# An edge-list kernel for four graph layers: layer 2 without its division, its norms and beta partly on GpSimd, and three tiles' gathers tied to earlier scores

## The chip, the cores and the metric

The kernel runs on one core of a Trainium2 chip. The core has a matrix engine (PE, TensorE), a vector engine (DVE, VectorE), an activation engine (ACT, ScalarE) and a general-purpose engine (POOL, GpSimd); SP (SyncE) issues most of the DMA transfers. Each engine works through its own queue in a fixed order and waits on semaphores for the others. The metric is the device time of one execution in microseconds (us), and a kernel's figure is the median of several executions.

## What is computed

Four residual graph layers on `x` of shape (8, 2048, 64) over one adjacency matrix of 2048 x 2048, which is sparse (about four neighbours for a node on average, many more for the first nodes). Each layer is `x = x + layer(max(layernorm(x), 0))`:

```python
# layer 0: dot-product attention, no weights
scores = einsum('bnd,bmd->bnm', h, h) / 8
x += softmax(where(adj > 0, scores, -1e12)) @ h
# layer 1: additive attention, elu
h1 = h @ W; e = leaky_relu(h1 @ a1 [rows] + h1 @ a2 [columns], 0.2)
x += elu(softmax(where(adj > 0, e, -9e15)) @ h1)
# layer 2: four dot-product heads with self loops, then one more such attention
def gat(h, mask, b): return softmax(where(mask, h @ h.T, -1e16)) @ h + b
z  = leaky_relu(concat_heads(gat(h @ Wh.T, adj + I, bh)), 0.2)
z2 = leaky_relu(gat(z @ Wo.T, adj + I, bo), 0.2)
x += (z2 - mean(z2)) * rsqrt(var(z2) + 1e-5) * gamma + beta
# layer 3: as layer 1, with relu in place of elu
```

A node with no neighbour at all gets the mean of all rows in layers 0, 1 and 3, since a softmax over equal masked scores is uniform.

## The kernel before

**Tiles.** The 2048 nodes are 16 tiles of 128, one node to a partition. A tile's row holds all eight batches side by side (`F` = 512 = 8 x 64). An edge list is built on the chip in layer 0 (`lists`, lines 594 to 718). After it, tile `i` has `ROWS[i]` row slots (a slot is one neighbour for each of the 128 nodes) and `PACKED[i]` packed slots, which hold the further neighbours of the nodes that have many; 0/1 matrices, `sel` and `selt`, tie a packed slot to its nodes through TensorE. `sel` lies in DRAM and is loaded again for the second attention of layer 2 (L880, one load of 2 MB).

**Tables and gathers.** Every layer writes the rows that its neighbours will need to a DRAM table (`store_rows`, L352) and then fetches a slot's 128 rows by an indirect DMA that GpSimd issues (`gather`, L244) into a ring of 26 slots. Tables 0, 1 and 4 have one more row, the mean of all rows. `store_rows` makes it: for each tile four products of 128 columns with `ones` (L357), whose sums VectorE adds to `acc` (L359, L361), and after the last tile a transpose, a copy and a DMA. A gather needs the whole table, the mean too where there is one.

**Stages and loops.** `pipeline(*stages)` calls the stages of a layer for the 16 tiles in a given `order`, a later stage one tile behind the one ahead of it. A list scheduler then fixes each engine's order from these calls and its own costs; so an edit also shifts neighbours. The stages are:
- layer 0 (0 to 365 us): lists and dot-product attention, one tile after the other, with layer 1's norm and projection behind it;
- layer 1 (365 to 595 us): additive attention, then layer 2's head projections;
- the heads of layer 2 (595 to 1152 us): `take2` gathers a tile's rows and fetches the query rows of its packed slots (`fetch`, L752, the tiles `qe`, four of them), `first2` makes scores on VectorE (L777, L781), `second2` the weighted sums (GpSimd L794 and L807, TensorE L801 and L809), `third2` and `fourth2` the output projection;
- the second attention of layer 2 (1152 to 1440 us), described next;
- layer 3 (1440 to 1595 us).

**The second attention.** For a tile, `take3` gathers its slots and loads its own rows. `first3` squares the rows on ScalarE (L889) and makes scores (L423 to L432; the tile's own score is subtracted in L894). `second3` sums the weights (S, in L902), takes their reciprocal (L903), and calls `weigh_sum`, which multiplies the gathered rows by their weights (`wg`, L381, GpSimd) and adds them up in PSUM with TensorE (`y`, L386). `third3` divides `y` by S (L472), adds the bias `bo` (L910), takes leaky relu (L445, L446) and begins the layer norm (`norm_a`: sum L261, mean L265, subtraction L268, square on ScalarE). `norm_b` (L281 to L286) ends it: a sum, then ScalarE's Ln and Exp for the reciprocal root. `fourth3` scales the tile (L292), multiplies by gamma (L918), adds beta (L919), adds to `x` (`add_store`, L486), stores `x`, and starts the layer norm for layer 3 with another `norm_a`. `pre_b`, `pre_c` (L313, four transposes L300, copy L301) and `pre_d` make layer 3's rows and store table 4.

**Small steps.** List building and the norms use many operations on 128 x 1 to 128 x 24 elements on VectorE (L645, L662, L664, L717, L718, L265, L273).

Of the kernel before, what the change touches and what calls it, by code (L numbers as in the profile page):

```python
# [65 lines left out]
def edge_stack(ctx: ExitStack, tc: tile.TileContext, x_in, adj, w1, w1t, a1, wh, wht, bh, wo, bo,  # L66
# [28 lines left out]
    nc.gpsimd.memset(eps, EPS)  # L95
    ones = const.tile([P, 1], F32, name="ones")
# [17 lines left out]
    acc = const.tile([P, F // P], F32, name="acc")  # L114

# [40 lines left out]
    bo_b, gamma_b, beta_b = (const.tile([P, D], F32, name=name) for name in ("bo_b", "gamma_b", "beta_b"))  # L156

    def weights_in(pool):
# [34 lines left out]
        for t, src in ((bo_b, bo), (gamma_b, gamma), (beta_b, beta)):  # L193
            nc.gpsimd.dma_start(out=t, in_=bass.AP(tensor=src.tensor, offset=src.offset, ap=[[0, P], [1, D]]))
# [62 lines left out]

    def norm_a(src, st, centre, eng=nc.vector):
# [4 lines left out]
        if centre:  # L263
            mean = small.tile([P, B], F32, name="ln_m")
            eng.tensor_scalar(mean, s, INV_D, None, op0=OP.mult)  # L265
            st["less"] = None
            st["src"] = rows_pool[0].tile([P, F], F32, name="ln_xc", bufs=3)
            eng.tensor_tensor(heads(st["src"]), heads(src), wide(mean), op=OP.subtract)  # L268
# [4 lines left out]
        nc.vector.tensor_scalar(st["less"], s, -INV_D, None, op0=OP.mult)  # L273
# [4 lines left out]
    def norm_b(st):  # L278
# [3 lines left out]
        nc.scalar.activation(q, q, AF.Ln, scale=INV_D, bias=eps)  # L282
# [12 lines left out]
    def transposed(src):  # L295
# [5 lines left out]
        nc.scalar.copy(t.rearrange("p k n -> p (k n)"), p)  # L301
# [5 lines left out]
    def pre_c(u, eng=None):  # L307
        def f(i, st):
# [6 lines left out]
            if u is not None:  # L315
                st["xt"] = transposed(st["xh"])
# [19 lines left out]
    def pre_d(k, u):  # L336

        def f(i, st):
# [8 lines left out]
            store_rows(k, i, xh, k != 2)  # L347
        return f

    def store_rows(k, i, xh, mean):  # L350
        cols = table[k].shape[1]
        nc.sync.dma_start(out=table[k][i * P:(i + 1) * P, :], in_=xh[:, :cols])  # L352
        if mean:
            C = F // P
            p = ps_m.tile([P, F], F32, name="m")
            for c in range(C):
                nc.tensor.matmul(p[:, c:c + 1], xh[:, c * P:(c + 1) * P], ones, start=True, stop=True)  # L357
            if i == order[0]:
                nc.vector.tensor_copy(acc, p[:, :C])  # L359
            else:  # L360
                nc.vector.tensor_tensor(acc, p[:, :C], acc, op=OP.add)  # L361
            if i == order[-1]:
                p = ps_m.tile([P, F], F32, name="m")
                nc.tensor.transpose(p[:C, :P], acc, ident)
                mr = rows_pool[0].tile([C, P], F32, name="mr", bufs=1)
                nc.vector.tensor_copy(mr, p[:C, :P])
                nc.sync.dma_start(out=table[k][N, :F].rearrange("(c p) -> c p", p=P), in_=mr)

# [4 lines left out]
    def weigh_sum(i, st, w, own=None, eng=nc.gpsimd):  # L373
# [3 lines left out]
        if own is not None:  # L377
            nc.tensor.matmul(y, ident, own, start=True, stop=False)
        for t0, m, g in rows(i, 0, n, 2):
# [133 lines left out]
    def additive(k, wd, *finish):  # L513
# [18 lines left out]
        def first(i, st):  # L532
# [6 lines left out]
            for t, m, g in rows(i, 0, K):  # L539
                nc.vector.tensor_tensor(s[:, t:t + m, :], g[:, :, F:], fs[:, None, :B].to_broadcast([P, m, B]),  # L540
                                        op=OP.add)
# [3 lines left out]
            if k == 4:  # L545
                nc.vector.tensor_tensor(s[:, :K, :], s[:, :K, :], fs[:, None, B:].to_broadcast([P, K, B]),
                                        op=OP.subtract)
# [33 lines left out]
    with tc.tile_pool(name="rows", bufs=2) as rp:  # L581
        rows_pool[0] = rp
        sel_all[0] = rp.tile([P, sum(PACKED) * P], F32, name="sel", bufs=1)
        with tc.tile_pool(name="lists", bufs=2) as pool, \
# [39 lines left out]
            def lists(i, st):  # L624
# [20 lines left out]
                nc.vector.tensor_scalar(ends, ends, LIFT, 0.0, op0=OP.subtract, op1=OP.max)  # L645
# [16 lines left out]
                nc.vector.tensor_scalar(idx[:, at:at + K], ell[:, :K], -1.0, N + 1.0, op0=OP.mult, op1=OP.add)  # L662
                if K > 1:
                    nc.vector.tensor_scalar(mba[:, at + 1:at + K], ell[:, 1:K], 0.0, NEG, op0=OP.is_equal, op1=OP.mult)  # L664
# [52 lines left out]
                nc.vector.tensor_scalar(idx[:, at + K:at + K + T], ke, -1.0, N + 1.0, op0=OP.mult, op1=OP.add)  # L717
                nc.vector.tensor_scalar(mp, mp, NEG, None, op0=OP.mult)  # L718
# [744 lines left out]
```

## Time and profile before

| what | us |
|---|---|
| median of three runs | 1600.91 (1598.85 to 1601.07) |
| the profiled execution | 1596.8 |
| its span, first to last instruction | 1595.0 |
| TensorE matmul busy in the span | 1295.0 |
| VectorE busy | 1242.0 |
| GpSimd busy | 1006.4 |
| ScalarE busy | 768.0 |
| mean granted TensorE clock (1 is full speed) | 0.899 |

The span and the profiled execution's own time differ by the 1.8 us that lie around the program. A busy time is the sum over an engine's instructions, without the issue of DMAs; where two engines are both busy, they overlap, so the column does not add up to the span. "Busy" also says nothing of what a stage waits for: that is read stage by stage, and from the chain of waits that leads to the last instruction. In lines of a group, `L472 DVE TENSOR_TENSOR y<-y,rec 128x512 ... x16 | 11.0, 690 | 2.4 <-PE y L386` means line 472 on VectorE, output and inputs, their size, sixteen instructions, 11.0 us in all, 690 ns for one, and 2.4 us of idle time of the engine ahead of them, with what ended most of it.

### The profile page before, as it was taken

What the parts mean: (1) busy time and instruction counts of PE and PEld (TensorE: products, weight loads), DVE (VectorE), ACT (ScalarE), POOL (GpSimd) and SP (SyncE); (2) the same over time, 40 slices, a digit from 0 to 9 for tenths busy, and PEclk for the clock granted to TensorE, in tenths of its full rate; (3) what the DMA queues carried; (4) which work ended last, traced back from release to release, by engine and by line L of the source; (5) the groups of instructions that cost most, each with busy time, mean ns of one, the idle gap of its engine ahead of it and who ended that gap; (6) DMA issues with size and microseconds to landing.
All of it is one profiled execution on the core that took longest, in us unless ns stands there. A gap on an engine that the chain in (4) does not pass through costs nothing.

```text
span 1595.0 us, 16633 instructions
## 1 busy us (share of the span) xinstructions
PE 1295.0 (81%) x4280; PEld 671.0 (42%) x4280; DVE 1242.0 (78%) x2489; ACT 768.0 (48%) x2475; POOL 1006.4 (63%) x844
## 2 busy tenths in 40 slices
PE   3768898995989771899987999999747788975888
PEld 1624354564544430344343444443323354563555
DVE  5998989854689776999998799871159999974666
ACT  3424555672557781465541455555424446680111
POOL 6336777766750007998789889898278486306650
PEclk9997887987999996899999999999968798957899
DMA  7775654536874449465266345400085354136761
GB/s 216 233 244 158 201 183 152 198 107 182 260 253 153 173 164 348 161 232 173 88 209 204 111 141 182 158 14 7 27 321 154 93 179 126 67 103 204 244 205 69
DMA packets 88177, 266.99 MB, mean 167 GB/s; under 512 B 14957, under 2 KB 15001, under 8 KB 79881
## 3 DMA queue, kind: packets, MB, share of 16 engines
q0 software_dynamic: 37392, 141.05, 28.3%
q1 hardware_dynamic: 50680, 124.80, 22.6%
q8 instruction: 36, 0.59, 0.2%
q14 instruction: 69, 0.56, 0.1%
HBM read 208.74 MB, written 57.05 MB: 167 GB/s over the span
## 4 chain that ended last, share of the span: by engine, by line
PE 24%; DVE 13%; POOL 8%; DMA 7%; ACT 6%; issue 5%; SPq 0%; POOLq 0%; DVEq 0%; ACTq 0%
PE y L809 10%; DMA g<-table,idx 4%; POOL wh L794 3%; POOL g L244 3%; DMA rows<-table 3%; PE y L386 3%; PE y L801 2%; PE m L846 2%; ACT yn L817 2%; PE m L858 2%; DVE s L781 2%; DVE prod L777 2%; DVE prod L423 1%; POOL wh L807 1%; PE m L842 1%
## 5 line engine op out<-in xcount | busy, mean ns | idle before, releaser
L244 POOL DMA_INDIRECT g<-table,idx x405 | 389.3, 961 | 268.3 <-issue 115.6
L794 POOL TENSOR_TENSOR wh<-g,w 128x1024 f32<-128x1024 f32 x162 | 307.2, 1918 | 35.8 <-PE y L809 33.9
L386 PE MATMUL y<-wg,ident 128*128 128x512 f32 x392 | 223.0, 696 | 22.6 <-POOL wg L381 12.7
L381 POOL TENSOR_TENSOR wg<-g,w 128x1024 f32<-128x1024 f32 (+1 forms) x91 | 156.6, 1736 | 75.2 <-ACT w L437 65.9
L781 DVE TENSOR_REDUCE s<-prod 128x32 f32<-128x2048 f32 x81 | 183.9, 2286 | 20.2 <-ACT w L783 19.8
L809 PE MATMUL y<-wh,ident 128*128 128x512 f32 x320 | 155.6, 614 | 23.7 <-POOL wh L807 21.5
L386 PE MATMUL y<-wg,selt 128*128 128x512 f32 x256 | 135.1, 634 | 4.6 <-POOL wg L381 2.9
L809 PE MATMUL y<-wh,selt 128*128 128x512 f32 x256 | 123.1, 605 | 13.2 <-POOL wh L794 13.2
L817 ACT ACTIVATE yn<-y,rec 128x64 f32<-128x64 f32 x512 | 111.3, 367 | 29.7 <-PE y L809 29.0
L386 PEld LDWEIGHTS y<-wg,ident 128*128 128x128 f32 x392 | 79.0, 219 | 106.6 <-issue 66.2
L777 DVE TENSOR_TENSOR prod<-q,g 128x2048 f32<-128x2048 f32 x49 | 111.5, 2275 | 3.7 <-ACT g L775 3.3
L381 DVE TENSOR_TENSOR wg<-g,w 128x1024 f32<-128x1024 f32 (+1 forms) x92 | 98.9, 1086 | 11.3 <-PE y L386 9.5
L443 DVE SCALAR_TENSOR_TENSOR zt<-m,bhc,att 128x512 f32<-128x512 f32 x64 | 47.1, 737 | 75.3 <-ACT att L442 75.3
L809 PEld LDWEIGHTS y<-wh,ident 128*128 128x128 f32 x320 | 59.4, 195 | 98.6 <-issue 62.4
L400 PE MATMUL m<-w,selt 128*128 128x8 f32 (+1 forms) x384 | 58.8, 255 | 50.7 <-ACT w L437 16.5
L400 PEld LDWEIGHTS m<-w,selt 128*128 128x128 f32 x384 | 60.8, 205 | 92.9 <-ACT w L437 26.8
L775 ACT COPY g<-g 128x512 f32<-128x512 f32 x81 | 50.4, 622 | 84.5 <-DVE prod L777 83.6
L429 PE MATMUL q<-rows,sel 128*128 128x512 f32 x128 | 79.8, 725 | 12.7 <-DVE prod L431 4.7
L801 PE MATMUL y<-rows,ident 128*128 128x512 f32 x128 | 70.9, 640 | 19.6 <-DMA rows<-table 14.4
L777 DVE TENSOR_TENSOR prod<-qe,g 128x2048 f32<-128x2048 f32 x32 | 73.0, 2281 | 13.9 <-DMA qe<-qtab,qidx 12.7
L357 PE MATMUL m<-ones,xh 128*128 128x1 f32 x384 | 70.6, 307 | 10.7 <-DVE idx L717 3.5
L357 PEld LDWEIGHTS m<-ones,xh 128*128 128x128 f32 x384 | 70.8, 274 | 20.0 <-issue 13.2
(221 smaller groups left out, 2673.0 us busy)
## 6 DMA issues: line engine op xcount, KB each, us to landing
qtab<-q SPq DMA_DIRECT2D x16, 1040.0 KB, 4.1
a<-in_adj_dram SPq DMA_DIRECT2D x32, 512.0 KB, 5.1
q<-qtab SPq DMA_DIRECT2D x14, 1040.0 KB, 5.3
table<-xh SPq DMA_DIRECT2D x48, 256.0 KB, 3.3
rows<-table SPq DMA_DIRECT2D x48, 256.0 KB, 4.1
xs<-x SPq DMA_DIRECT2D x48, 256.0 KB, 2.2
x<-xs SPq DMA_DIRECT2D x48, 256.0 KB, 3.3
table<-xh SPq DMA_DIRECT2D x32, 260.0 KB, 2.1
```

The source lines that it names most:

```text
L244: g = nc.gpsimd.indirect_dma_start(out=ring[:, (held[i] + t) % RING, :cols], out_offset=None, in_=table[k][:, :], in_offset=bass.IndirectO ...
L357: nc.tensor.matmul(p[:, c:c + 1], xh[:, c * P:(c + 1) * P], ones, start=True, stop=True)
L381: eng.tensor_tensor(wg[:, :m].rearrange("p t (b d) -> p t b d", b=B), g[:, :, :F].rearrange("p t (b d) -> p t b d", b=B), w[:, t0:t0 + m, ...
L386: nc.tensor.matmul(y, lhs(i, t), wg[:, t - t0, :], start=(t == 0 and own is None), stop=(t == n - 1))
L400: nc.tensor.matmul(p[:, :cols], selt(i, t), packed[:, t, :], start=(t == 0), stop=(t == T - 1))
L429: nc.tensor.matmul(qe, sel(i, t - K), q, start=True, stop=True)
L777: nc.vector.tensor_tensor(pr.rearrange("p (b h) d -> p b h d", h=H), q[:, :B * H * D].rearrange("p (b h d) -> p b h d", h=H, d=D), heads(g ...
L781: nc.vector.tensor_reduce(s[:, t - lo, :], pr, AX.X, OP.add)
L794: nc.gpsimd.tensor_tensor(wg, heads(row(i, t))[:, :, None, :].to_broadcast([P, B, 2, D]), w[:, :, 2 * k:2 * k + 2, None].to_broadcast([P, ...
L801: nc.tensor.matmul(st["ys"][j], ident, xb[:, 4 * j:4 * j + 4], start=True, stop=False)
L809: nc.tensor.matmul(st["ys"][j], lhs(i, t), wg[:, 4 * j:4 * j + 4], start=False, stop=(t == n - 1))
L817: nc.scalar.activation(yn[:, b, h, :], st["ys"][j][:, b, h, :], AF.Copy, scale=st["rec"][:, 4 * j + b, 2 * k + h:2 * k + h + 1])
```

## The change

It has five parts.

1. **Small steps.** Twelve kinds of `tensor_scalar` or `tensor_tensor` on VectorE whose operands lie in SBUF become `scalar_tensor_tensor` with the same result; the second operand is then a constant tile (`zero`, `np1`, `neg1`) read as a broadcast, or the operation itself.
2. **Means.** `store_rows` makes none. For table 0 the old way stays, called earlier. For table 1, the copy after the transposes becomes four ScalarE copies that sum as they go (`accum_out`, into `parts`), with one reduction at the end. For table 4, one product `ones` x `xh` of 1 x 512 adds up over the tiles in a PSUM bank.
3. **Second attention of layer 2.** `y` is no longer divided by S: layer norm does not depend on the scale of its input if the constant 1e-5 is scaled by S squared, and leaky relu keeps a positive factor. So `rec` is now 1e-5 x S x S, added to the variance in `norm3`, and the bias enters `y` as S x bo, by a product of the transposed S (8 x 128) with a block-diagonal `bo_d`. Beta is added to `x` by GpSimd (`beta3`) and not behind gamma, and the mean and the subtraction of the norm of `x` move to GpSimd.
4. **`sel`** is loaded in 16 pieces, each behind the load of its tile's rows.
5. **Heads.** In `take2` the first gather of the fifth, sixth and seventh tile waits for the last score of the tile four ahead.

```diff
@@ constants
+    zero, np1, neg1 = (const.tile([P, 1], F32, name=name) for name in ("zero", "np1", "neg1"))
+    for t, v in ((zero, 0.0), (np1, N + 1.0), (neg1, NEG)):
+        nc.gpsimd.memset(t, v)
+    parts = const.tile([P, NT, F // P], F32, name="parts")
@@ new helpers
+    def alike(t, like):
+        return t.to_broadcast(like.shape)
+    def times(dst, src, k):
+        nc.vector.scalar_tensor_tensor(dst, src, k, alike(zero, src), op0=OP.mult, op1=OP.add)
+    def less_from(dst, src):
+        nc.vector.scalar_tensor_tensor(dst, src, -1.0, alike(np1, src), op0=OP.mult, op1=OP.add)
@@ norm_a
-            eng.tensor_scalar(mean, s, INV_D, None, op0=OP.mult)
+            if eng is nc.vector:
+                times(mean, s, INV_D)
+            else:
+                eng.tensor_scalar(mean, s, INV_D, None, op0=OP.mult)
...
-            eng.tensor_tensor(heads(st["src"]), heads(src), wide(mean), op=OP.subtract)
+            if eng is nc.vector:
+                nc.vector.scalar_tensor_tensor(heads(st["src"]), heads(src), 1.0, wide(mean), op0=OP.mult,
+                                               op1=OP.subtract)
+            else:
+                eng.tensor_tensor(heads(st["src"]), heads(src), wide(mean), op=OP.subtract)
...
-        nc.vector.tensor_scalar(st["less"], s, -INV_D, None, op0=OP.mult)
+        times(st["less"], s, -INV_D)
@@ norm_b
-    def norm_b(st):
+    def norm_b(st, more=None):
...
-        nc.scalar.activation(q, q, AF.Ln, scale=INV_D, bias=eps)
+        if more is None:
+            nc.scalar.activation(q, q, AF.Ln, scale=INV_D, bias=eps)
+        else:
+            nc.vector.scalar_tensor_tensor(q, q, INV_D, more, op0=OP.mult, op1=OP.add)
+            nc.scalar.activation(q, q, AF.Ln)
@@ transposed
-        nc.scalar.copy(t.rearrange("p k n -> p (k n)"), p)
+        if part is None:
+            nc.scalar.copy(t.rearrange("p k n -> p (k n)"), p)
+        else:
+            for k in range(F // P):
+                nc.scalar.activation(t[:, k, :], p[:, k * P:(k + 1) * P], AF.Copy, accum_out=part[:, k:k + 1])
@@ pre_c(u, eng=None, k=None)
-                st["xt"] = transposed(st["xh"])
+                st["xt"] = transposed(st["xh"], parts[:, i, :] if k == 1 else None)
+            if k is not None:
+                mean_of(k, i, st["xh"])
@@ store_rows keeps only the store; the rest becomes mean_of
+    def mean_of(k, i, xh):
+        if k == 4:
             if i == order[0]:
+                kept["mean"] = ps_w[0].tile([P, F], F32, name="w")
+            p = kept["mean"]
+            nc.tensor.matmul(p[:1, :], ones, xh[:, :F], start=(i == order[0]), stop=(i == order[-1]))
             if i == order[-1]:
+                mr = rows_pool[0].tile([1, F], F32, name="mr", bufs=1)
+                nc.vector.tensor_copy(mr, p[:1, :])
+                nc.sync.dma_start(out=table[k][N:N + 1, :F], in_=mr)
+            return
...
+        if k == 1:
+            if i == order[-1]:
+                nc.vector.tensor_reduce(acc, parts.rearrange("p i c -> p c i"), AX.X, OP.add)
                 p = ps_m.tile([P, F], F32, name="m")
                 nc.tensor.transpose(p[:C, :P], acc, ident)
                 mr = rows_pool[0].tile([C, P], F32, name="mr", bufs=1)
-                nc.vector.tensor_copy(mr, p[:C, :P])
+                nc.scalar.mul(mr, p[:C, :P], 1.0 / N)
                 nc.sync.dma_start(out=table[k][N, :F].rearrange("(c p) -> c p", p=P), in_=mr)
+            return
...
@@ weigh_sum
+        if more is not None:
+            nc.tensor.matmul(y, *more, start=False, stop=False)
@@ lists
-                nc.vector.tensor_scalar(ends, ends, LIFT, 0.0, op0=OP.subtract, op1=OP.max)
+                nc.vector.scalar_tensor_tensor(ends, ends, LIFT, alike(zero, ends), op0=OP.subtract, op1=OP.max)
...
-                nc.vector.tensor_scalar(idx[:, at:at + K], ell[:, :K], -1.0, N + 1.0, op0=OP.mult, op1=OP.add)
+                less_from(idx[:, at:at + K], ell[:, :K])
...
-                nc.vector.tensor_scalar(mp, mp, NEG, None, op0=OP.mult)
+                times(mp, mp, NEG)
@@ take2
-            gather(2, i, st)
+            n = order.index(i)
+            gather(2, i, st, taken[2, order[n - 4]] if 4 <= n < 7 else None)
@@ score
-                nc.vector.tensor_tensor(s[:, t - lo, :], s[:, t - lo, :], q[:, B * H * D:], op=OP.subtract)
+                taken[2, i] = nc.vector.tensor_tensor(s[:, t - lo, :], s[:, t - lo, :], q[:, B * H * D:], op=OP.subtract)
@@ second attention of layer 2
-        nc.sync.dma_start(out=sel_all[0], in_=sel_dram[:, :])
+        bo_d = rp.tile([B, F], F32, name="bo_d", bufs=1)
+        nc.sync.dma_start(out=heads(bo_d), in_=bass.AP(tensor=bo.tensor, offset=bo.offset, ap=[[0, B], [0, B], [1, D]]))
+        nc.gpsimd.affine_select(out=heads(bo_d), in_=heads(bo_d), compare_op=OP.is_equal, fill=0.0, base=0,
+                                pattern=[[-1, B], [0, D]], channel_multiplier=1)
@@ take3
+            mine = slice(POFF[i] * P, (POFF[i] + PACKED[i]) * P)
+            nc.sync.dma_start(out=sel_all[0][:, mine], in_=sel_dram[:, mine])
@@ first3
-            nc.vector.tensor_tensor(s[:, :K], s[:, :K], c[:, None, :].to_broadcast([P, K, B]), op=OP.subtract)
+            nc.vector.scalar_tensor_tensor(s[:, :K], s[:, :K], 1.0, c[:, None, :].to_broadcast([P, K, B]),
+                                           op0=OP.mult, op1=OP.subtract)
@@ second3
-            nc.vector.scalar_tensor_tensor(seen[:, i, :], p, 1.0, d, op0=OP.add, op1=OP.add)
-            nc.vector.reciprocal(rec, seen[:, i, :])
-            st["y"] = weigh_sum(i, st, w, st["rows"])
+            S = seen[:, i, :]
+            nc.vector.scalar_tensor_tensor(S, p, 1.0, d, op0=OP.add, op1=OP.add)
+            nc.vector.scalar_tensor_tensor(rec, S, EPS, S, op0=OP.mult, op1=OP.mult)
+            p = ps_m.tile([P, F], F32, name="m")
+            nc.tensor.transpose(p[:B, :P], S, ident)
+            sums = small.tile([B, P], F32, name="sums")
+            nc.scalar.copy(sums, p[:B, :P])
+            st["y"] = weigh_sum(i, st, w, st["rows"], more=(sums, bo_d))
@@ third3
-            divide(st, y)
-            nc.vector.tensor_tensor(heads(y), heads(y), over_d(bo_b), op=OP.add)
@@ fourth3 and behind it
-            nc.vector.tensor_tensor(heads(p), heads(p), over_d(beta_b), op=OP.add)
-            add_store(i, st, p, True)
-        pipeline(take3, first3, second3, third3, both(pre_b, xs_rows), fourth3, pre_b, pre_c(u3), pre_d(4, u3))
+            add_store(i, st, p, True, eng=nc.gpsimd)
+        def norm3(i, st):
+            norm_b(st, st["rec"])
+        def beta3(i, st):
+            nc.gpsimd.tensor_tensor(heads(st["x"]), heads(st["x"]), over_d(beta_b), op=OP.add)
+        pipeline(take3, first3, second3, third3, both(norm3, xs_rows, beta3), fourth3, pre_b, pre_c(u3, None, 4), pre_d(4, u3))
         bounds(4, seen)
+        nc.vector.tensor_scalar(most[:, 4:5], most[:, 4:5], 1e15, None, op0=OP.mult)
```

The same swap to `scalar_tensor_tensor` is made in L540, L546 (its first operand) and L664. The last line scales one of the bounds that are compared at the end, so that S squared stays within range.

## The prediction

> **What bounds the kernel now.** I read first the busy time by stretch, cut at the stages that the loops make: layer 0, layer 1, layer 2's heads, layer 2's second attention (a start, a body and an end of it), layer 3. Columns: the stretch, its length, then busy us (and instructions) of PE, PEld, DVE, ACT and POOL, granted clock, DMA share, GB/s.
>
> ```profile
> 76.00:352.00 276.00, 229.75 (x809) 123.92 (x809) 240.89 (x835) 147.81 (x514) 195.01 (x174) 0.87 0.55 178
> ...
> 595.00:1152.00 557.00, 481.65 (x1357) 207.95 (x1355) 433.86 (x381) 266.33 (x841) 458.05 (x293) 0.96 0.43 147
> 1152.00:1190.00 38.00, 13.93 (x32) 6.63 (x32) 16.08 (x30) 7.31 (x18) 26.95 (x28) 0.67 0.90 328
> 1190.00:1403.00 213.00, 174.32 (x574) 93.04 (x574) 203.05 (x387) 119.05 (x414) 132.00 (x100) 0.85 0.40 123
> 1403.00:1440.00 37.00, 27.20 (x101) 21.02 (x101) 22.40 (x45) 26.33 (x100) 0.98 (x1) 0.50 0.28 94
> ```
>
> No engine bounds the whole. In 1190 to 1403 VectorE is busy 203 of 213 us: that body is VectorE's. Its start is the DMA engines' (0.90), its end a chain of short steps at clock 0.50. Layer 0 leans on VectorE (241 of 276), the heads on TensorE (482 of 557) with GpSimd close behind. The second attention is where most of the edit lands, so next its groups in 1190 to 1403:
>
> ```profile
> L472 DVE TENSOR_TENSOR y<-y,rec 128x512 f32<-128x512 f32 x16 | 11.0, 690 | 2.4 <-PE y L386 2.4
> ...
> L910 DVE TENSOR_TENSOR y<-y,bo_b 128x512 f32<-128x512 f32 x15 | 10.3, 688 | 0.0
> ...
> L268 DVE TENSOR_TENSOR ln_xc<-x,ln_m 128x512 f32<-128x512 f32 x12 | 9.5, 792 | 0.0
> ...
> L919 DVE TENSOR_TENSOR q<-q,beta_b 128x512 f32<-128x512 f32 x12 | 8.2, 686 | 0.0
> ...
> L381 POOL TENSOR_TENSOR wg<-g,w 128x1024 f32<-128x1024 f32 (+1 forms) x45 | 77.3, 1734 | 60.8 <-ACT w L437 55.7 <-PE y L386 4.9
> L244 POOL DMA_INDIRECT g<-table,idx x55 | 55.1, 1002 | 15.8 <-issue 10.0 <-POOL wg L381 2.1 <-DVE q L919 0.6
> ```
>
> The first four are steps the change takes from VectorE. The last two are all that GpSimd does there; it idles 60.8 us ahead of wg, mostly for the weights w. Then the chain of waits at the two places where a queue is reordered: the start of the second attention, and of the heads (start us, us, what).
>
> ```profile
> 1154.38 0.32 SPq L880
> ...
> 1156.33 15.52 DMA rows<-table
> ...
> 1171.93 17.83 DMA rows<-table
> ...
> 1189.78 0.64 ACT sq L889
> ```
> ```profile
> 627.00 0.94 POOL g L244
> ...
> 628.25 7.94 DMA qe<-qtab,qidx
> 636.22 2.30 DVE prod L777
> ```
>
> At 1154 one 2 MB load of sel (8.2 us to landing) goes ahead of the rows; the row loads behind it take 15 and 18 us, and the first compute on rows starts at 1165.3. In the heads 26 gathers at 1.25 us stand ahead of the first qe load on GpSimd; VectorE idles 12.7 us for it.
>
> **Two rules weighed.** The Trainium skill, "SBUF — State Buffer", section "Who interferes with whom", says that a VectorE instruction with two SBUF inputs waits for a GpSimd instruction that reads SBUF, and that tensor_scalar can wait too, through a two-port mode. The rows:
>
> ```profile
> L313 DVE SCALAR_TENSOR_TENSOR xh<-ln_xc,ln_r x16: 661/680/995, 31.8 to 69.8; 128x512 f32<-128x512 f32 x16
> L664 DVE TENSOR_SCALAR mba<-ell x14: 136/157/3745, 27.8 to 266.4; 128x2 f32<-128x2 f32 x6, 128x1 f32<-128x1 f32 x5, 128x8 f32<-128x8 f32 x1, 128x5 f32<-128x5 f32 x1
> 43.45 0.99 DVE L313 SCALAR_TENSOR_TENSOR xh<-ln_xc,ln_r 128x512 f32<-128x512 f32 x1
> 42.85 1.04 POOL L268 TENSOR_TENSOR ln_xc<-x,ln_m 128x512 f32<-128x512 f32 x1
> ```
>
> L664, two to eight columns, is 0.16 us at the median and up to 3.75: it does wait. But L313 is just the new form, a scalar_tensor_tensor with two SBUF inputs, and it waits too: at 43.45 it takes 0.995, ending 0.55 after the GpSimd step that ends at 43.89. The trace agrees with the page, so I go by it: rewriting tensor_scalar with a constant from SBUF doesn't escape GpSimd. The second, "TensorE: Matmul & The Clock Gate", section "What's actually happening": an idle array is throttled and a busy one released. The trace agrees: 0.50 and 0.67 in the sparse stretches, 0.96 in the heads. So TensorE work that fills gaps costs less than its time at 0.85.
>
> **The change part by part.**
> *Second attention, body, VectorE.* Gone in the stretch: L472 11.0, L910 10.3, L919 8.2, L268 on x 9.5, half of L265's 5.1 (2.5), L903 2.9, L361 and L359 1.7: 46.1. Added: the rec and the q steps, some 29 of 0.155 (L902's form): 4.5. Net -41.6.
> *GpSimd there* takes on the x norms, 12 x (1.04 L268 + 0.27 L265) = 15.7, and about 14 beta adds at 1.27 (L480) = 17.8: +33. It has 132 + 55 gathers x 0.3 between issues = 148.5; new 182. Queued behind a beta or norm that waits (for the load of x, for VectorE's sum) are the wg products and gathers; TensorE's y waits for those.
> *TensorE there:* the means of table 4 go (88 of L357, 11.8); one 1x512 product in two passes comes for 11 tiles, and for 15 tiles the bias product in two passes and an 8-row transpose. At 0.57 a pass (L386: 56.0/98): 12.5 + 17 + 15 x 0.3 = 34. Net +22: 196 at clock 0.85, about 167 at the heads' 0.49 a pass (L809: 155.6/320).
> So VectorE needs 161, GpSimd 182, TensorE 167 to 196. Three in-order queues that feed each other don't all run full. Bounds: 41.6 gained if VectorE stays the only limit, none if TensorE takes 213 at its old density. I take 198: **-15**.
> *Its start.* sel comes in 16 pieces behind the rows. The first rows need not wait 8.2 us, but gathers and loads fill the DMA engines to 1190 all the same: 0 to -8, **-5**. More SP issues, 16 for 1 at 0.32, lie beside full DMA engines. The bias load and its mask on GpSimd are two single steps under the gathers: nothing, or 3 us if the mask's DMA is late.
> *Its end.* Each of the last tiles spends 1.84 on L357 between transposes at clock 0.50; now about 1.1 and no acc or transpose. Three tiles x 0.7, and 2 at the mean's end, less 0.5 for the norm on the slower GpSimd: **-4** (-1 to -7). The first `w` in layer 3 shares the mean's bank, and its gathers wait for the mean anyhow.
> *Layer 0.* The mean of table 1 leaves TensorE (106 of L357 after 208 us, about 0.13 us each beside their loads) for ScalarE: four 128x128 copies that sum, about 0.37 each by interpolating L292 (335 for 64 columns) and L301 (581 for 512), instead of one of 0.58: +0.9 a tile, +0.3 if each sum needs a read like L711's 81 ns. ScalarE has 148 of 276, so it is hidden; uncovered it costs 14 to 19. The end of the layer (352 to 365, the same L357 chain) gains about 3; TensorE's relief 2: **-5**.
> *The small steps.* Their excess over the median in layer 0: L664 10.1, L645 5.6, L718 3.2, L662 2.6, L717 2.0: 23. Bounds: all 23 gone; or, since the 23 one-column steps that never waited now have two SBUF inputs, 23 x 0.4 = 9 lost. By L313 I take **0**. In layers 1 and 3 the same edit has no GpSimd product beside it: 0.
> *The heads.* The first gathers of the fifth to seventh tile move behind the qe loads: three of 1.25, qe 3.75 earlier. They come back in GpSimd's dense part, and their wait (scores four tiles earlier) is over by then. 0 to -4, or +4 if GpSimd pays and TensorE waits: **-2**. A planner sets the order, so other neighbours shift a little: +-5 anywhere.
> Sum: -15 -5 -4 -5 -2 = **-31**. The profiled execution took 1596.8 (span 1595.0); that gives 1565.8, and against the median 1600.9, **1570**.
>
> **Rivals.** *VectorE alone counts:* TensorE's clock rises, GpSimd keeps up, and all 41.6 show: 26 more, **1544**. For it: clock 1.00 in dense stretches. Against: GpSimd's 182. *The next engine takes over at once:* the body gains 3, layer 0 and the heads nothing: -12, **1589**. For it: TensorE's 196. *The slower one: GpSimd as a gate.* It had 64.5 us free in the body; 33 more leave 31. If the 12 norm pairs wait over 31/12 = 2.6 us each, GpSimd outlasts the old 213. Its present waits average 5 us (60.8 in 12); at 5 each 60 - 31 = 29 are added, less 16 gained elsewhere: **1614**. For it: norms wait for VectorE, which they didn't before. Against: the 60.8 us that it idles for w overlaps these waits. *The waits stay but the small steps go through:* the 23 of layer 0 vanish, held in the range.
>
> **How the numbers follow.** 1570 (1556 to 1584): 0.50. 1544: 0.14. 1589 (1584 to 1600): 0.20. 1614 (over 1600): 0.16. The range 1544 to 1604 leaves out half of the second case and 0.13 above. Faster by over 0.2% (under 1597.7; 0.2% is what a measurement of this kernel can tell from no change) 0.83, within it 0.04 (0.01 of the third case, 0.03 of the fourth), slower 0.13.
>
> **What would show it.** Right: the stretch from the first sq to the last norm of the second attention near 198 us, VectorE near 165 busy in it, GpSimd near 165 plus issue gaps, TensorE's clock above 0.85; rows landing before 1160; small steps in layer 0 still with maxima of 2 to 4 us. Wrong: GpSimd waiting for ln_s or x by tens of us and y's products for wg; layer 0 shorter by 20; or the body still 210 with TensorE full.

## The result: slower by 1.3%, and the profile after

The changed kernel takes 1620.7 us (median of four, 1618.41 to 1623.64) against 1599.88 for the kernel before beside it: ratio 1.0131, 95% interval 1.0111 to 1.0151. The forecast was 1570. The profiled execution has a span of 1619.8 us, 24.8 more than before.

Where the time went is read from stages cut at the same event in both traces: the first gather of a stage to the first gather of the next (for layer 3, to its last gather).

| stage (us) | before | after | difference |
|---|---|---|---|
| layer 0 | 288.3 | 288.1 | -0.2 |
| layer 1 | 230.6 | 232.1 | +1.5 |
| heads of layer 2 | 559.4 | 561.9 | +2.5 |
| second attention of layer 2 | 283.8 | 304.8 | +21.0 |
| layer 3 | 115.8 | 115.4 | -0.4 |

So the loss lies in the stage in which the gain was forecast. Busy time by stretch of the changed kernel, columns as in the prediction (stretch, its length, then busy us of PE, PEld, DVE, ACT, POOL, granted clock, DMA share, GB/s); the three lines are the start, the body and the end of the second attention:

```profile
1156.00:1194.00 38.00, 24.43 (x49) 11.73 (x50) 24.36 (x40) 9.48 (x23) 28.88 (x29) 0.63 0.87 304
1194.00:1430.00 236.00, 198.03 (x542) 88.10 (x541) 200.91 (x317) 125.11 (x439) 164.00 (x140) 0.83 0.37 115
1430.00:1464.00 34.00, 24.15 (x70) 12.06 (x68) 15.73 (x26) 22.56 (x84) 5.41 (x9) 0.58 0.31 106
```

The body grew from 213 to 236 us. VectorE is as busy as it was (200.9 against 203.1), although the forecast had counted 46 us of work taken from it, and now idles 35 us where it idled 10. TensorE is busy 24 us more; its idle time stayed at 38. The groups of that body that answer to the lines of before (in the changed kernel `rec` is L966, its use in the norm L305, mean and subtraction of the norm of z L266 and L285, `wg` L433, the norm of x on GpSimd L281 and L288, beta L989, the bias product L430):

```profile
L285 DVE SCALAR_TENSOR_TENSOR ln_xc<-z,ln_m 128x512 f32<-128x512 f32 x14 | 18.6, 1331 | 0.3
...
L966 DVE SCALAR_TENSOR_TENSOR rec<-seen 128x8 f32<-128x8 f32 x13 | 15.9, 1220 | 0.1
L305 DVE SCALAR_TENSOR_TENSOR ln_q<-ln_q,rec 128x8 f32<-128x8 f32 x14 | 10.3, 735 | 0.2
...
L266 DVE SCALAR_TENSOR_TENSOR ln_m<-ln_s,zero 128x8 f32<-128x8 f32 x14 | 7.8, 554 | 0.1
...
L433 POOL TENSOR_TENSOR wg<-g,w 128x1024 f32<-128x1024 f32 (+1 forms) x44 | 75.3, 1724 | 26.7 <-ACT xh L316 8.9 <-PE y L438 8.3 <-ACT w L489 7.4
...
L989 POOL TENSOR_TENSOR x<-x,beta_b 128x512 f32<-128x512 f32 x13 | 16.4, 1268 | 7.6 <-DMA x<-xs 7.6
...
L281 POOL TENSOR_SCALAR ln_m<-ln_s 128x8 f32<-128x8 f32 x12 | 2.8, 232 | 19.7 <-DVE ln_s L274 17.7 <-DVE row L456 1.4
...
L430 PE MATMUL y<-bo_d,sums 8*128 8x512 f32 x28 | 19.7, 788 | 0.4 <-ACT sums L970 0.4
```

Two of these groups stood in the kernel before too, with the same number of steps on z:

```profile
L268 DVE TENSOR_TENSOR ln_xc<-z,ln_m 128x512 f32<-128x512 f32 x14 | 10.4, 740 | 0.0
...
L265 DVE TENSOR_SCALAR ln_m<-ln_s 128x8 f32<-128x8 f32 x26 | 5.1, 222 | 0.0
```

`rec`, an operation on 128 x 8 elements that takes 0.155 us when nothing holds it, averages 1.22. One of them in the timeline (start us, us, engine, line):

```profile
1351.27 1.05 POOL L288 TENSOR_TENSOR ln_xc<-x,ln_m 128x512 f32<-128x512 f32 x1
1351.42 5.84 DVE L966 SCALAR_TENSOR_TENSOR rec<-seen 128x8 f32<-128x8 f32 x1
1352.27 3.75 POOL L433 TENSOR_TENSOR wg<-g,w 128x1024 f32<-128x1024 f32 x2
1355.98 1.25 POOL L989 TENSOR_TENSOR x<-x,beta_b 128x512 f32<-128x512 f32 x1
...
1358.52 1.22 PE L481 MATMUL q<-rows,sel 128*128 128x512 f32 x1 [7.16 <-DVE prod L483]
1358.59 0.68 ACT L489 ACTIVATE w<-s,mbb 128x8 f32<-128x8 f32 x3 [8.58 <-DVE s L955]
```

`rec` starts while GpSimd subtracts, and ends (1357.26) within 0.04 us of the end of the fourth GpSimd operation in an unbroken row (1357.23). Meanwhile TensorE stands for 7.16 us and ScalarE for 8.58. The Trainium skill, "SBUF — State Buffer", section "Who interferes with whom", states a rule that fits: a VectorE instruction with two SBUF inputs contends with a GpSimd one that reads SBUF, since its second input comes through a shared port. The trace agrees: all 23 steps of L966, L305 and L266 in the second attention that took over 0.2 us longer than their usual time ended 0.02 to 0.04 us after a GpSimd operation did. How many operations a step waits for varies. Of the ten waits of these lines and L285 that met a row of several, six lasted to the row's end; four ended inside the row, like this one, 0.02 us after the first of two (each took half of the 3.76 us):

```profile
1265.42 3.76 POOL L433 TENSOR_TENSOR wg<-g,w 128x1024 f32<-128x1024 f32 x2 [3.59 <-ACT w L489]
1266.63 0.72 DVE L305 SCALAR_TENSOR_TENSOR ln_q<-ln_q,rec 128x8 f32<-128x8 f32 x1
```

What decides between the two is not shown.

The other place is the beginning of a tile's sum `y`. First the tile of 17 slots in the kernel before, in the timeline: the products of `wg` start on TensorE at 1259.07, while the sum of weights S comes only at 1278.59.

```profile
1259.07 1.88 PE L386 MATMUL y<-wg,ident 128*128 128x512 f32 x4
...
1278.59 0.15 DVE L902 SCALAR_TENSOR_TENSOR seen<-m,row 128x8 f32<-128x8 f32 x1
...
1295.44 1.02 PE L386 MATMUL y<-wg,selt 128*128 128x512 f32 x2
```

Then the same tile in the changed kernel: S, its transpose, its copy, the bias product, and only then `wg`.

```profile
1281.22 0.16 DVE L965 SCALAR_TENSOR_TENSOR seen<-m,row 128x8 f32<-128x8 f32 x1
...
1283.29 0.42 PE L968 MATMUL m<-ident,seen 128*8 128x128 f32 x1
...
1284.08 0.24 ACT L970 COPY sums<-m 8x128 f32<-8x128 f32 x1
...
1284.37 2.07 PE L430 MATMUL y<-bo_d,sums 8*128 8x512 f32 x2 [0.42 <-ACT sums L970]
...
1286.37 2.08 PE L438 MATMUL y<-wg,ident 128*128 128x512 f32 x2
...
1315.12 6.65 PE L438 MATMUL y<-wg,selt 128*128 128x512 f32 x10
```

S needs all weights of the tile. Standing ahead of the `wg` products in the sum, the bias product makes all of them wait for it. `y` of this tile is complete at 1321.8 instead of 1296.5; counted from the first gather of the stage, S came 1.2 us earlier than before (122.3 against 123.5) and `y` 21.5 us later (162.8 against 141.3).

### The profile page after: what moved, and what is told of

It is laid out like the page before. It is cut to its first block, busy times and chain, and to the rows that moved or that the text cites. A ratio compares the mean times of both kernels' runs of the same rounds, so it can differ in the third digit from the quotient of the medians.

```text
span 1619.8 us, 16343 instructions
## 1 busy us (share of the span) xinstructions
PE 1313.8 (81%) x4103; PEld 645.3 (40%) x4103; DVE 1241.3 (77%) x2394; ACT 779.4 (48%) x2604; POOL 1048.0 (65%) x895
## 5 line engine op out<-in xcount | busy, mean ns | idle before, releaser
L433 POOL TENSOR_TENSOR wg<-g,w 128x1024 f32<-128x1024 f32 (+1 forms) x91 | 155.7, 1722 | 33.5 <-ACT w L489 10.3
L438 PE MATMUL y<-wg,selt 128*128 128x512 f32 x256 | 139.8, 653 | 4.4 <-DVE wg L433 3.3
L864 PE MATMUL y<-wh,selt 128*128 128x512 f32 x256 | 126.3, 620 | 10.6 <-POOL wh L849 10.6
L433 DVE TENSOR_TENSOR wg<-g,w 128x1024 f32<-128x1024 f32 (+1 forms) x92 | 98.9, 1087 | 10.3 <-PE y L438 8.3
L481 PE MATMUL q<-rows,sel 128*128 128x512 f32 x128 | 83.1, 747 | 24.0 <-DVE prod L483 16.1
L856 PE MATMUL y<-rows,ident 128*128 128x512 f32 x128 | 70.5, 639 | 22.7 <-DMA rows<-table 15.5
L832 DVE TENSOR_TENSOR prod<-qe,g 128x2048 f32<-128x2048 f32 x32 | 73.0, 2282 | 11.3 <-DMA qe<-qtab,qidx 9.5
L357 PE MATMUL q<-q,xt 128*128 128x512 f32 x128 | 65.8, 620 | 16.6 <-DVE prod L359 11.0
L901 PE MATMUL m<-att,whd 128*128 128x512 f32 x128 | 68.4, 616 | 11.7 <-ACT att L899 11.7
```

The lines of the kernel that those rows point to most:

```text
L433: eng.tensor_tensor(wg[:, :m].rearrange("p t (b d) -> p t b d", b=B), g[:, :, :F].rearrange("p t (b d) -> p t b d", b=B), w[:, t0:t0 + m, ...
L438: nc.tensor.matmul(y, lhs(i, t), wg[:, t - t0, :], start=(t == 0 and own is None), stop=(t == n - 1))
L481: nc.tensor.matmul(qe, sel(i, t - K), q, start=True, stop=True)
L832: nc.vector.tensor_tensor(pr.rearrange("p (b h) d -> p b h d", h=H), q[:, :B * H * D].rearrange("p (b h d) -> p b h d", h=H, d=D), heads(g ...
L856: nc.tensor.matmul(st["ys"][j], ident, xb[:, 4 * j:4 * j + 4], start=True, stop=False)
L864: nc.tensor.matmul(st["ys"][j], lhs(i, t), wg[:, 4 * j:4 * j + 4], start=False, stop=(t == n - 1))
```

## The experiments

All kernels of a group ran on one chip, with the kernel before beside them. On some chips the kernel before takes 1643 us, on others 1600. Two traces of it show where: layer 1 takes 230.6 or 250.7 us and layer 3 115.8 or 133.4, while layer 0, the heads and the second attention agree within 0.5 us. So a ratio is compared within a group; the changed kernel itself was repeated only in the second one. Across groups the second attention's stage time is compared, which two traces of the changed kernel gave as 304.8 and 305.9. It comes from one execution, which lay up to 9.5 us from its kernel's median: bias_last and bias_last_sums differ by 0.2 us in their medians and by 5.6 in this column. Differences of that size are not read as effects. "Excess" below is the time that VectorE's instructions in the second attention take over the lower quartile of their own kind and shape: some 8 and 11 us in the two traces of before, 44 and 38 in those of the changed kernel.

| kernel | ratio to before (95% interval) | second attention, us | excess, us |
|---|---|---|---|
| before | 1 | 283.8, 284.2 | 8, 11 |
| changed | 1.0131 (1.0111 to 1.0151) | 304.8 | 44 |
| x_on_vector | 1.0062 (1.0039 to 1.0085) | 298.9 | 15 |
| sums_apart | 1.0108 (1.0073 to 1.0143) | 305.9 | 13 |
| both_apart | 1.0129 (1.0082 to 1.0176) | 315.4 | 12 |
| old_steps | 1.0115 (1.0059 to 1.0171) | 307.0 | 32 |
| after_again | 1.0138 (1.0098 to 1.0177) | 305.9 | 38 |
| bias_last | 1.0047 (1.0032 to 1.0061) | 291.7 | 35 |
| no_bias | 0.9994 (0.9980 to 1.0007) | 282.6 | 28 |
| bias_last_sums | 1.0041 (1.0026 to 1.0057) | 297.3 | 22 |
| bias_last_x | 0.9981 (0.9966 to 0.9996) | 291.1 | 27 |
| bias_last_both | 1.0056 (1.0039 to 1.0073) | 301.4 | 16 |
| bias_last_heads | 1.0009 (0.9994 to 1.0024) | 294.4 | 35 |
| division_back | 1.0068 (1.0042 to 1.0095) | 297.3 | 19 |
| division_back_sel | 1.0080 (1.0055 to 1.0105) | 300.5 | 19 |
| division_back_mean | 1.0118 (1.0061 to 1.0174) | 303.6 | 18 |
| bias_last_x_heads | 1.0015 (0.9993 to 1.0036) | 291.2 | 27 |
| swap_alone | 1.0172 (1.0117 to 1.0227) | 301.9 | 17 |
| division_back_old | 0.9994 (0.9971 to 1.0018) | 295.5 | 14 |

**First group: the waits of the small steps, or GpSimd's queue?** The norm of x and beta back on VectorE (x_on_vector):

```diff
             nc.vector.tensor_tensor(heads(p), heads(p), over_d(gamma_b), op=OP.mult)
-            add_store(i, st, p, True, eng=nc.gpsimd)
+            nc.vector.tensor_tensor(heads(p), heads(p), over_d(beta_b), op=OP.add)
+            add_store(i, st, p, True)
...
-both(norm3, xs_rows, beta3)
+both(norm3, xs_rows)
```

> The changed kernel with the norm of x and beta back on VectorE (beta behind gamma, as before); everything else as changed. Queue theory (GpSimd's queue in order is the gate: its waits for ln_s and for x, 27 us in the second attention, hold the products wg behind them): those waits go, 1590 to 1602 us. Port theory (VectorE's small steps with two SBUF operands stand until GpSimd pauses; 43 us of excess in the second attention where before had 6.5): 20 us of work come back to VectorE, and the excess falls with the 33 us of GpSimd work that leave, to about 30: little net, 1612 to 1626 us.

`rec` and the variance without two SBUF operands (sums_apart), and both edits (both_apart):

```diff
-            nc.vector.scalar_tensor_tensor(rec, S, EPS, S, op0=OP.mult, op1=OP.mult)
+            nc.scalar.activation(rec, S, AF.Square, scale=EPS ** 0.5)
...
-        nc.vector.tensor_reduce(q, heads(st["sq"]), AX.X, OP.add)
+        qs = q if more is None else st["pn"][:, :B]
+        nc.vector.tensor_reduce(qs, heads(st["sq"]), AX.X, OP.add)
...
-            nc.vector.scalar_tensor_tensor(q, q, INV_D, more, op0=OP.mult, op1=OP.add)
+            nc.vector.scalar_tensor_tensor(q, qs, INV_D, more, op0=OP.mult, op1=OP.add)
...
+            st["pn"] = ps_q.tile([P, F], F32, name="q")
             norm_b(st, st["rec"])
```

> The changed kernel with the two new small steps kept from needing two SBUF operands: rec = 1e-5 S S by a Square on ScalarE, and the variance summed into PSUM, so that its step with rec has one SBUF operand. Port theory: the 18 us of excess of rec and the 8 us of ln_q go, 1594 to 1603 us, and both steps measure 0.15 to 0.3 us each. Queue theory: the gate stays, 1615 to 1625 us.

> Both edits together: norm of x and beta on VectorE, rec on ScalarE, variance in PSUM. If both causes add: 1575 to 1592 us, faster than before. Queue theory alone: as x_on_vector, 1590 to 1602. Port theory alone: as sums_apart or 5 to 10 above it, for 20 us more VectorE work less the excess that leaves with GpSimd's: 1594 to 1606.

And part 1 undone, every `scalar_tensor_tensor` of it as it was before (old_steps):

> The changed kernel with part 1 undone: the small steps that were there before (lists, norms, scores) are tensor_scalar and tensor_tensor again; rec and ln_q stay. Port theory: both forms wait for GpSimd, so the layer 0 excess (16.5 us before, 21.6 changed) returns to about 17 and the second attention keeps most of its 43: 1610 to 1620 us. A rival, that the new form itself is the loss: 1600 to 1608 us. Queue theory: 1617 to 1624 us.

x_on_vector gets back about half of the loss (1.0062 against 1.0131 and 1.0138 on other chips), less than the queue theory asked, though its excess falls to 15, below the 30 of the port theory. sums_apart does to its steps what it should, as the summary of its variance step shows (minimum, median, maximum in ns), and yet the stage is not shorter. Its waits from 1194 to 1430 us of its trace (total us, times, longest) show where the time went: VectorE now stands for 32 us in three waits behind leaky relu, which waits for `y`; in the changed kernel that wait is 10.6 us.

```profile
L306 DVE SCALAR_TENSOR_TENSOR ln_q<-q,rec x16: 148/156/167, 1220.0 to 1456.3; 128x8 f32<-128x8 f32 x16
```
```profile
DVE z L499 <- ACT att L498: 32.2, 3, 19.3
DVE seen L966 <- PE m L453: 14.4, 4, 5.1
```

both_apart missed all three of its forecasts; its stage is the longest of all, 315.4. So neither theory explains the loss: in sums_apart what VectorE saves turns into a wait for `y`. (The edit also holds a PSUM bank one stage longer, from the norm on; what that costs was not tried apart, so the price of the small steps' waits is bounded by these runs, not measured.) old_steps stays at 1.0115, where the port theory had it: in the changed kernel the form of the small steps has no effect that shows.

**Second group: the order of the sum.** bias_last moves one product:

```diff
-        if more is not None:
-            nc.tensor.matmul(y, *more, start=False, stop=False)
...
-                                 stop=(t == n - 1))
+                                 stop=(t == n - 1 and more is None))
+        if more is not None:
+            nc.tensor.matmul(y, *more, start=False, stop=True)
```

> The changed kernel unaltered, so that its trace and ratio stand beside the next three on the same chip. All theories: ratio to before 1.010 to 1.016, as measured first.

> The changed kernel with the bias product S x bo as the last product of y and not ahead of the products of wg. Order theory (the bias product needs S, so all weights of a tile; standing ahead in TensorE's queue it keeps the wg products back, which before began up to 20 us before S was known; the wg buffers then hold GpSimd): the products of wg begin before S again for the tile of 17 slots, and 15 to 28 us come back: ratio to before 0.995 to 1.004. Load theory (TensorE's 24 us more work in the second attention is the loss): ratio unchanged, 1.010 to 1.015. Port theory: unchanged too.

no_bias calls `weigh_sum(i, st, w, st["rows"])` without the transpose, the copy, the product and `bo_d`.

> The changed kernel without the bias bo of the second attention: no transpose of S, no copy, no product, no bo_d. It leaves that addition out. Order theory: as the bias-last kernel, and 0 to 8 us faster than it by the TensorE time saved. Load theory: 20 us of TensorE work go, 15 to 20 us faster than the bias-last kernel. Port theory: no change from 1.013.

> Bias product last, and rec on ScalarE and the variance in PSUM as in sums_apart. If the order hid what the waits of the small steps cost: 5 to 20 us faster than the bias-last kernel alone, ratio to before 0.983 to 0.998. If those waits cost nothing: the same as the bias-last kernel within 3 us.

On one chip, 1.0138 becomes 1.0047: the place of this one product costs 0.9%, some 14 us, both in the ratio and in the stage (305.9 to 291.7), just under the 15 us that the order theory asked at least. The tile of 17 slots in the timeline of bias_last: its `wg` products (here L436) again start 15 us ahead of S (L965), and the bias product (L439) ends `y` at 1307.2, 148.4 us after the stage's first gather.

```profile
1262.94 1.98 PE L436 MATMUL y<-wg,ident 128*128 128x512 f32 x4 [0.74 <-POOL wg L431]
...
1277.57 0.15 DVE L965 SCALAR_TENSOR_TENSOR seen<-m,row 128x8 f32<-128x8 f32 x1
...
1306.06 1.12 PE L439 MATMUL y<-bo_d,sums 8*128 8x512 f32 x2
```

Without the bias 8 us more go by the medians and 9 in the stage (291.7 to 282.6), at the edge of the 0 to 8 of the order theory and less than the 15 to 20 of the load theory, and the stage is as long as before. So the bias product accounts for the 21 us: 14 by where it stood, 8 to 9 by being there. Still, this kernel has neither division nor bias and is no faster than before: of the 24 us forecast for this stage (15, 5 and 4) nothing shows. The whole stage of before and of no_bias:

```profile
1155.10:1439.00 283.90, 215.45 (x707) 120.70 (x707) 241.53 (x460) 152.61 (x529) 158.97 (x128) 0.78 0.45 148
1159.40:1442.10 282.70, 213.38 (x610) 99.37 (x610) 227.02 (x381) 151.81 (x529) 198.33 (x176) 0.80 0.46 148
```

VectorE's busy time there fell by 14.5 us only, in part since its excess rose to 28, and it now idles 56 us where it idled 42. Which wait took these 14 us was not tried. bias_last_sums again takes excess from VectorE (35 to 22) and gains nothing (1607.2 against 1607.0 us).

**Third group: what is left with the bias last, and parts 1, 2 and 4 alone.** bias_last_x, bias_last_both and bias_last_heads join edits shown above; bias_last_heads also calls `gather(2, i, st)` without its wait. division_back puts back the division, the bias on VectorE, the norm's constant, the place of norm and beta, and the heads' gathers: parts 1, 2 and 4 remain.

> Bias product last, and the norm of x and beta back on VectorE. Queue theory as a second cause (betas and norms ahead of wg and gathers on GpSimd, 8 us at the second tile's first product alone): 6 to 14 us faster than the bias-last kernel, ratio to before 0.995 to 1.001. If the order was all: VectorE gets 20 us more work, ratio 1.003 to 1.012.

> Bias product last, norm of x and beta on VectorE, rec on ScalarE, variance in PSUM. With GpSimd relieved VectorE is the limit again, and the small steps' waits count: 3 to 10 us faster than the kernel with bias last and x on VectorE, ratio 0.988 to 0.998. If VectorE isn't the limit there either: the same within 3 us.

> Bias product last, and part 5 undone (no gather in the heads waits for scores). If the gather waits cost what the heads lost (4 us between the 225th and the 240th gather): ratio 1.001 to 1.003, and the heads end 3 to 5 us earlier. If the planner's other order is the cause: the heads stay, ratio 1.0047 as with bias last.

> Parts 1, 2 and 4 of the change alone (small steps, means, sel in pieces): division, bias, beta and norms on VectorE and the heads' gathers as before. By the prediction's terms for these parts (start -5, end -4, layer 0 -5): 1586 us, ratio 0.989 to 0.994. If they bring nothing, as the stages of the changed kernel suggest (layer 0 ends at the same time): ratio 0.997 to 1.003.

With the bias last, the place of norm and beta no longer shows in the stage (291.1 against 291.7). By its ratio bias_last_x is where the queue theory as a second cause had it, and its interval is the one that lies below 1, by 0.04% at its upper end; but bias_last itself was not run on this chip, and a like kernel with the heads' waits taken out came to 1.0015. So no gain is claimed, and a cost of some us by the place of norm and beta is not excluded. bias_last_both is longer again. Over all kernels the heads take 558.9 to 560.6 us without the gather waits and 559.9 to 562.5 with them: part 5 gained nothing, and its loss is 1 us in the mean. Unforeseen was division_back: three parts that were to gain 14 us cost 0.7%, with the second attention 13 us longer.

**Fourth and fifth group: which of parts 1, 2 and 4.** division_back_sel loads sel whole; division_back_mean makes table 4's mean the old way; swap_alone is the kernel before with part 1; division_back_old is division_back with the old small steps.

> The kernel before, unaltered, for a trace on the same chip as the next three. Its second attention (255th to 330th gather) takes 276 us if the chips differ only in layers 1 and 3, 285 or more if the chip slows this stage too.

> Parts 1 and 2 alone: the division-back kernel with sel loaded whole, ahead of the rows. If the 16 pieces cost the 13 us that the second attention lost there (issues on SP between the loads of rows and x): the stage returns to 276 to 280 us, ratio 0.998 to 1.002. If the mean of table 4 is the cause: ratio 1.005 to 1.010.

> Parts 1 and 4 and the mean of table 1: the division-back kernel with the mean of table 4 by the old four products for a tile, acc and transpose. If the 1 x 512 products (0.95 us a tile at the clock of this stage, ahead of other tiles' products in TensorE's queue) cost the 13 us: the stage returns to 276 to 280 us, ratio 0.998 to 1.002. If sel in pieces is the cause: 1.005 to 1.010.

> Bias product last, norm of x and beta on VectorE, no gather wait in the heads. If the gather waits cost 2 to 4 us in the heads: ratio 0.9955 to 0.997, and the heads (165th to 240th gather) take 379 to 380 us, as before. If they cost nothing: 0.998 as without this edit.

> The kernel before with part 1 alone (small steps as scalar_tensor_tensor). If the new form costs the 13 us that parts 1, 2 and 4 lost in the second attention: 280 to 288 us from the 255th to the 324th gather where before takes 269, ratio 1.004 to 1.009. If both forms wait alike, as the trace before suggested: 267 to 272 us, ratio 0.998 to 1.002; the loss then comes with the means or sel, whichever way they are made, through the planner's order.

> Parts 2 and 4 alone: the division-back kernel with the small steps in their old form. If part 1 costs the 13 us: 267 to 273 us in the second attention (255th to 324th gather), ratio 0.995 to 1.001. If parts 2 and 4 bring it through the planner's order: 278 to 286 us, ratio 1.003 to 1.009.

Neither sel nor the mean is the cause; putting each back made the stage 3 to 6 us longer. Then the two halves: against before_again, of the same chip, part 1 alone has layer 0 longer by 12.2 us and the second attention by 17.7, and costs 1.7%; parts 2 and 4 alone have layer 0 shorter by 4.3 and the second attention longer by 11.3, with the other stages within 1, and their ratio is 0.9994. (The stages are those of single profiled executions, 1642.6 us for parts 2 and 4 and 1633.3 for before_again, whose median beside it was 1642.8; so some of these 11 us may be scatter.) But part 1's cost is not its waits alone: the excess in layer 0 is 19.8 us in swap_alone and 22.7 and 16.5 in the two traces of before, and in the second attention 17 against 8 and 11, some 8 of the 18 lost. Nor do the parts add up. Together (division_back) parts 1, 2 and 4 have the second attention 13 us longer and not 29; taking part 1 out of them shortens layer 0 by 10 us and the second attention by 2; taking it out of the changed kernel (old_steps) gains nothing in either.

What else differs is the order. Compared with before by the longest sequence of VectorE instructions that both traces have in the same order (instructions told apart by tiles and shapes), some 460 of swap_alone's 2489 fall outside it, though the edit changes only their form; between two traces of one kernel none does. The planner costs the new form differently and lays the queues out anew. But a new order need not cost anything: against the changed kernel some 380 of 2394 fall outside in old_steps, which takes as long, and 130 in bias_last. No experiment held the order fixed, so what part 1 costs by itself, and how a cost splits between order and waits, stays open; and the same caution holds for differences under some 10 us among these kernels.

## Why the prediction was wrong, step by step

- **The body of the second attention (-15) is the step that failed.** It measured +23. Its weighing, "Three in-order queues that feed each other don't all run full", with bounds from VectorE's saving to none, left out a dependency. The bias product was costed as TensorE time ("the bias product in two passes", 17 us; it took 19.7) and not as a wait, although the diff puts it ahead of the `wg` products of its sum and it needs S. bias_last shows what that was worth: 14 us. The body lies 38 us off its forecast: 14 by this wait, 8 to 9 by the bias product's own time, and the remaining 15 or so are the gain that stays away even without a bias.
- **TensorE and GpSimd were sized right.** 196 us forecast for TensorE, 198.0 measured; 182 for GpSimd, 164.0 busy and 59 gathers with 0.3 us between issues measured, 181.7. The clock did not rise (0.83), so TensorE's added work showed: no_bias is 9 us shorter than bias_last.
- **VectorE's net of -41.6 was mis-sized by its added terms.** "Some 29 of 0.155", 4.5 us, measured 15.9 + 10.3 = 26.2 for 27 instructions. The same page had been weighed ahead of it, and L313 shown to wait with two SBUF operands; the rule was applied to the old small steps and not to the two new ones. With 13 us more on L285 and L266 (18.6 + 7.8 against 10.4 and 14 x 0.22 before), 39 us of VectorE's work came back. By sums_apart this alone did not set the time; that the forecast gain is missing without the bias too (no_bias) is not explained by any run.
- **The start (-5) was right in size and lost again.** The first tile's `wg` products begin 32.3 us after the stage's first gather, 37.8 before. But six beta adds (7.5 us) then stand ahead of gathers on GpSimd, and the second tile's products begin at 49.2 instead of 43.3.
- **The end (-4)** measured -7.5 from the last `wg` product to layer 3's first gather (38.7 to 31.2), just outside its range.
- **Layer 0 (-5)** measured -0.2, and -2.9 in the second pair of traces. The means' term is not contradicted by division_back_old against before_again (-4.3), but two traces of the changed kernel differ by 3.2 here. The small steps' waits stayed (22.7 before, 24.4 after), as argued from L313; what the forecast lacked is that a change of form also reorders the queues (swap_alone's layer 0 is 12 us longer without more waits). What ate the means' gain here is not shown.
- **The heads (-2)** measured +2.5; "other neighbours shift a little: +-5 anywhere" was too narrow for the two stages that hold most small steps.
- **The rivals.** GpSimd as a gate, 1614, is nearest by its number, and what the prediction named as a sign of being wrong, GpSimd waiting for ln_s or x by tens of us, was there: 19.7 us for ln_s and 7.6 for x, 2.3 a pair, just under the 31/12 from which it was to decide. Yet x_on_vector, which removes them, returns about half, and with the bias last the stage gains nothing by it. So its number was near for another reason: it aggravated the loss with the bias product first, and was not its main cause.

## What to carry to other kernels

A product in a PSUM sum has a place as well as a price: put the operand that is ready last at the end of the sum, since everything behind it in TensorE's queue waits with it. Before moving work off the busiest engine, follow one tile's chain through the new operations and ask which old overlap they end; here 39 of the 46 us of VectorE time that were to go came back in four groups of small steps, and VectorE's idle time grew from 10 to 35 us. Where a planner orders the queues, a change of form is a change of order, so a small edit has to be measured by itself, and parts measured alone need not add up.

## What the runs showed of the hardware

- A VectorE step of 0.155 us with two SBUF operands took up to 5.84 us beside GpSimd, through four operations without a pause. With one operand in PSUM the variance step took 148 to 167 ns in all 16 cases, eight of which ran beside a GpSimd operation on SBUF; the page cited above states that a VectorE instruction with at most one SBUF input does not contend, outside the two-port modes.
- A pass of an 8-row product of 512 columns takes 587 ns at its fastest and 692 at the median (L430), about what the passes of the 128-row products of `wg` take (592 at their fastest and at the median): a shallow product saves no time. The Trainium skill, "TensorE: Matmul & The Clock Gate", section "Why this matters for your kernels", states the same for 32 rows.
- On some chips the two layers whose table rows have 520 columns take 18 to 20 us longer, the stages with rows of 512 columns not at all. This rests on two traces of before, one on a chip of each kind; what differs there was not tried.
